# Layer 0's first head: four unread products in place of five, and its Toeplitz matrix loaded in two halves from two issuing engines

## The chip, the cores and the metric

The kernel runs on one core of a Trainium2 chip. The metric is the device time of one execution in microseconds (us); the time of a kernel is the median of its runs. "The profile" is one execution recorded by the hardware profiler: a page of sums, and a trace that can be asked for single instructions. Engines: PE is TensorE's matmul and PEld its weight load, DVE is VectorE, ACT is ScalarE, POOL is GpSimd, SP is SyncE. A "q" behind a name (SPq, ACTq) marks a DMA issue by that engine.

## The reference

An array x of 64 batches, 32 heads (positions) and 512 features goes through two layers, each a "conditioning" step and a feed-forward step that are added to x. The change touches only the conditioning step of layer 0, a long convolution along the 512 features with one kernel per head:

```python
def _get_kernel(log_dt, C, log_A_real, A_imag, length):
    Cc = C[..., 0] + 1j * C[..., 1]
    dt = jnp.exp(log_dt)
    A = -jnp.exp(log_A_real) + 1j * A_imag
    dtA = A * dt[:, None]
    P = dtA[:, :, None] * jnp.arange(length, dtype=jnp.float32)
    Cs = Cc * (jnp.exp(dtA) - 1.0) / A
    K = 2.0 * jnp.einsum('hn,hnl->hl', Cs, jnp.exp(P)).real
    return K
...
u_m = u * mask[:, None, :]
kernel = _get_kernel(log_dt, C, log_A_real, A_imag, Lq)
...
y = jnp.fft.irfft(u_f * k_f, n=n)[..., :Lq]
y = y + u_m * D[:, None]
return y * mask[:, None, :]
```

After it come a mixture of low-rank adapters beside a dense product (layer 0's feed-forward), a gated layer with adapters per batch (layer 1's conditioning) and a mixture of 16 experts with a shared one (layer 1's feed-forward).

## The kernel before, in words

All arithmetic is float32. x lies in SBUF transposed (`xall`, features on partitions), and layer 0 works on it in four blocks `tb` of eight heads each.

*The convolution kernels.* For each block of heads the 512 values of the kernel of each head are made from exponentials and sines (class `Kernels`: `decays`, `angles`, `weighed` on VectorE and ScalarE), then a small product per head on TensorE (`products`, L329). `to_memory` copies the result out of PSUM (L334), adds D to the first value (L336) and stores it in a DRAM tensor `kpad` with a DMA that ScalarE issues (L338). A row of `kpad` is 127 zeros and the 512 values. The first block is split: `early` makes heads 0 to 5, `second` heads 6 and 7.

*The unread products.* Between them stand five products of 128 x 512 (L400) whose result nobody reads; they are written into `ps_mm`, the PSUM pool that the convolutions use too. A float32 product of this kernel is recorded as two weight loads and two matmuls ("passes").

*The convolution.* `convolved(tb, hl, yT)` loads for two heads at a time the Toeplitz matrices `g` (L495): partition p of head h reads 512 values of `kpad` that begin at p. Heads 0 and 1 come as two loads of 256 KB, later pairs as one of 512 KB; the tile has three buffers. Then head h's product y is four matmuls, one for each block d of 128 columns of g (L511), and VectorE multiplies y with the length mask into `yT` (L518). Behind each head come two steps of the next block's kernels (the first is `decays`, L306 and L307). After eight heads `by_tokens` (L528) and the main products (L589) take yT.

*What sets the order.* Inside `tc.manual_schedule(engines=by_hand)` the instructions of PE, DVE and Activation keep the order in which they are written, DMA issues included. SP and POOL are put in order by the scheduler. The written order around the change is: `early.products()`, `early.to_memory()`, the angles of `second`, the unread products, `second.products()`, `second.to_memory()`, and then, in the loop over `tb`, `convolved(0, 0, yT)`.

Of the kernel before, what the change touches and what calls it, by code (L numbers as in the profile page):

```python
# [17 lines left out]
P = 128  # L18
B, H, L = 64, 32, 512
# [15 lines left out]
KW = 640  # L35
# [68 lines left out]
def kernel(ctx: ExitStack, tc: tile.TileContext, a: dict, out: bass.AP):  # L104
    nc = tc.nc
# [11 lines left out]
    def bank(pool, name):  # L117
        return pool.tile([P, TB], F32, tag="bank", name=name)
# [62 lines left out]
    kpad = dram.tile([H, KW], F32, name="kpad")  # L181
# [14 lines left out]
    def fetch(n):  # L196

        g, j = divmod(n, NF)
        blocks[n] = stream.tile([P, 7 * BW], F32, tag="w", name=f"w_{n}")
        if g == 0:  # L200
            nc.sync.dma_start(blocks[n][:, 0 : 4 * BW], a["cw"][j])
        else:
            nc.sync.dma_start(blocks[n][:, 0 : 3 * BW], a["cw"][j][:, 0 : 3 * BW])
            nc.sync.dma_start(blocks[n][:, 3 * BW :], sums_d[j])
# [191 lines left out]
        ts(mlen[:, j, :], intf[:, 0, :], col(C_L + j), None, ALU.is_gt)  # L396
    run(second.weighed())

    for _ in range(5):
        mm(bank(ps_mm, "unread"), ident, xT[0][:, 0, :], start=True, stop=True)  # L400
    second.products()
    second.to_memory()
# [70 lines left out]
    with tc.tile_pool(name="l0", bufs=1) as l0, tc.tile_pool(name="l0b", bufs=2) as l0b:  # L473
# [10 lines left out]
        def convolved(tb, hl, yT):  # L484

            h = tb * HB + hl
            if h % 2 == 0:
                g = l0b.tile([P, 2, L], F32, tag="g", name=f"g_{h}", bufs=3)  # L490

                for i, n in ((0, 1), (1, 1)) if h == 0 else ((0, 2),):
                    src = kpad.offset + (h + i) * KW
                    src = bass.AP(tensor=kpad.tensor, offset=src, ap=[[1, P], [KW, n], [1, L]])
                    load = nc.sync.dma_start(g[:, i : i + n, :], src)  # L495
                if hl == HB - 2 and tb > 0:
                    with tc.issue_after(load.ins):
                        for n in ((0, 1), (2, 3), ())[tb - 1]:
                            fetch(n)
                        for j in range((tb - 1) * 4, min(tb * 4, NF)):  # L500
                            nc.sync.dma_start(wn[:, j, :, TW : TW + L // 2], a["cn"][j])
                if h == HB - 2:
                    with tc.issue_after(load.ins):
                        for later in range(1, NTB):
                            nc.sync.dma_start(xT[later], a["xT"][later])
                toeplitz.append(g)
            g = toeplitz[-1]
            y = bank(ps_mm, f"y_{h}")
            cols = slice(hl * B, (hl + 1) * B)
            for d in range(NC):  # L510
                mm(  # L511
                    y[:, d * B : NC * B],
                    g[:, h % 2, d * P : (d + 1) * P],
                    xT[tb][:, 0 : NC - d, cols],
                    start=(d == 0),
                    stop=(d == NC - 1),
                )
            tt(yT[:, :, cols], y[:, 0 : NC * B].rearrange("p (c b) -> p c b", b=B), mlen, ALU.mult)  # L518
            if tb in (1, 2):
                coming[0].rows(1)  # L520
# [80 lines left out]
        for tb in range(NTB):  # L601
# [7 lines left out]
            for hl in range(HB):  # L609
                convolved(tb, hl, yT)  # L610
                next(steps, None)
                next(steps, None)
                if hl == 1 and tb > 0:
                    counted(tb - 1)
                if tb == NTB - 1:
                    for j in range(hl, NF, HB):
                        columns(0, j)
# [328 lines left out]
    for g in range(NG):  # L946
# [3 lines left out]
        for j in range(NF):  # L950
# [6 lines left out]
            if j % 4 == 0:  # L957
                lo = adapters[:, 0 : min(4, NF - j)]
# [592 lines left out]
```

## Time and profile before

| | |
|---|---|
| median of 3 runs | 1020.14 us (1019.03 to 1020.51) |
| the profiled execution | 1020.05 us |
| its span, first to last instruction | 1018.3 us |
| mean granted TensorE clock | 1.000 |
| busy: PE, DVE, ACT, POOL | 987.4, 648.3, 212.0, 170.1 us |
| bytes moved by DMA | 190.62 MB, mean 187 GB/s |

The profiled execution's time is 1.75 us longer than its span; that is what lies around the first and the last instruction. Times inside the trace are counted from the span's start. A line of the timeline gives start, length, engine, line of the code, operation, what is written and read, shapes, how often in a row, and in brackets how long the engine had been idle and what ended that. Matmuls are pipelined, so their lengths overlap; the distance between starts is the better measure of their pace. DMA lines give the size of one transfer and the median time from its issue to its landing.

### The profile page before, as it was taken

The page shows a single profiled execution, that of the slowest core. Times are in us where ns is not written, and L with a number is a line of the kernel's source. Part 1 is how long each engine was busy: PE and PEld are TensorE (multiplying, and loading weights), DVE is VectorE, ACT ScalarE, POOL GpSimd, SP SyncE. Part 2 cuts the span into 40 slices and gives each one's busy share as a digit, 9 for nine tenths or more (in the row PEclk, how much of TensorE's full clock was granted, in tenths as well). Part 3 has the DMA queues.
Part 4 walks back from the last instruction along what each step waited for, and adds up shares of the span by engine and source line. Part 5 has one row for each costly group of instructions (what it writes and reads, how often), then busy time and mean ns, then how long its engine had stood idle before and what let it go on. Part 6 is the DMA issues. An engine that isn't in the chain of part 4 may idle for free. (4 is left out here: it accounts for less than half of the span.)

```text
span 1018.3 us, 16926 instructions
## 1 busy us (share of the span) xinstructions
PE 987.4 (97%) x6256; PEld 792.2 (78%) x6256; DVE 648.3 (64%) x1974; ACT 212.0 (21%) x439; POOL 170.1 (17%) x189
## 2 busy tenths in 40 slices
PE   3999999999999999999999999999999999999998
PEld 1777656888988889988889888897767677776665
DVE  6656567887666776766676767765765353333775
ACT  2322111121221311213212122121201222221100
POOL 2131001210301202102012021000000333331730
PEclk9999999999999999999999999999999999999999
DMA  6566408685665646746567557540940455555652
GB/s 187 191 224 232 136 21 301 236 294 174 224 199 192 238 164 213 248 161 214 186 198 257 175 189 238 172 141 17 409 188 1 133 167 166 166 165 199 200 176 95
DMA packets 64210, 190.62 MB, mean 187 GB/s; under 512 B 8512, under 2 KB 11616, under 8 KB 63488
## 3 DMA queue, kind: packets, MB, share of 16 engines
q1 hardware_dynamic: 49360, 138.30, 39.2%
q0 software_dynamic: 14176, 51.16, 16.2%
q8 instruction: 52, 0.85, 0.3%
q14 instruction: 30, 0.25, 0.1%
q10 hardware_dynamic: 592, 0.07, 0.1%
HBM read 158.35 MB, written 31.15 MB: 186 GB/s over the span
## 5 line engine op out<-in xcount | busy, mean ns | idle before, releaser
L885 PE MATMUL zp<-wn,at 128*128 128x288 f32 x704 | 185.4, 406 | 0.4 <-DVE at L984 0.4
L819 PE MATMUL gu<-t,w 128*128 128x128 f32 x1056 | 150.1, 278 | 0.9 <-DVE gus L966 0.9
L885 PEld LDWEIGHTS zp<-wn,at 128*128 128x128 f32 x704 | 127.1, 190 | 28.6 <-DVE at L984 0.6
L819 PEld LDWEIGHTS gu<-t,w 128*128 128x128 f32 x1056 | 135.4, 192 | 14.8 <-DVE gus L966 6.4
L444 POOL DMA_INDIRECT wa<-in_la,row_a x64 | 61.2, 956 | 299.9 <-issue 183.4
L982 ACT ACTIVATE si<-gus 128x256 f32<-128x256 f32 x88 | 36.7, 417 | 350.5 <-DVE gus L980 350.5
L819 PE MATMUL gum<-xall,w 128*128 128x128 f32 x704 | 93.0, 275 | 0.0
L819 PEld LDWEIGHTS gum<-xall,w 128*128 128x128 f32 x704 | 85.7, 192 | 0.0
L1327 PE MATMUL egu<-wall,zx 128*128 x336 | 80.6, 383 | 0.4 <-issue 0.4
L966 DVE TENSOR_TENSOR gus<-gu,los 128x512 f32<-128x512 f32 x88 | 60.6, 688 | 28.7 <-PE gu L819 26.2
L960 DVE TENSOR_TENSOR los<-los 128x512 f32<-128x512 f32 (+1 forms) x72 | 46.6, 647 | 49.9 <-ACT los L839 48.3
L1327 PEld LDWEIGHTS egu<-wall,zx 128*128 128x128 f32 x336 | 60.5, 189 | 20.0 <-ACT zx L1318 13.0
L984 DVE TENSOR_TENSOR at<-si,gus 128x256 f32<-128x256 f32 x88 | 37.4, 425 | 48.2 <-ACT si L982 48.2
L1308 POOL DMA_INDIRECT zr<-zd,tok x42 | 39.7, 946 | 159.4 <-PE zrp L1316 86.3
L839 ACT COPY los<-lo 128x512 f32<-128x512 f32 (+1 forms) x96 | 46.6, 560 | 60.1 <-PE lo L836 60.1
L1099 PE MATMUL op<-sat,sw 128*128 128x512 f32 x128 | 58.0, 595 | 0.6 <-DVE sat L1124 0.3
L589 PE MATMUL main<-yT,w 128*128 128x512 f32 x128 | 58.4, 599 | 0.0
L836 PEld LDWEIGHTS lo<-rs,wb 64*128 64x128 f32 x704 | 42.6, 187 | 16.0 <-issue 10.6
L836 PE MATMUL lo<-rs,wb 64*128 64x128 f32 x704 | 48.0, 279 | 6.1 <-DVE gus L980 5.5
L819 PE MATMUL gum<-t,w 128*128 128x128 f32 x352 | 53.7, 275 | 0.0
L819 PE MATMUL gu<-xall,w 128*128 128x128 f32 x352 | 53.7, 275 | 0.0
L1347 DVE COPY eys<-ey 128x512 f32<-128x512 f32 x42 | 29.1, 692 | 29.7 <-PE ey L1345 29.7
(316 smaller groups left out, 1452.0 us busy)
## 6 DMA issues: line engine op xcount, KB each, us to landing
w<-sums_d SPq DMA_DIRECT2D x77, 512.0 KB, 4.8
w<-in_cw SPq DMA_DIRECT2D x77, 384.0 KB, 3.4
wall<-in_xw SPq DMA_DIRECT2D x16, 768.0 KB, 15.1
yd<-eys SPq DMA_DIRECT2D x42, 256.0 KB, 2.8
g<-kpad SPq DMA_DIRECT2D x15, 512.0 KB, 5.5
w<-in_cw SPq DMA_DIRECT2D x11, 512.0 KB, 4.7
sums_d<-w SPq DMA_DIRECT2D x9, 512.0 KB, 3.6
xall<-in_xT SPq DMA_DIRECT2D x4, 1024.0 KB, 8.6
```

The lines of the kernel that those rows point to most:

```text
L444: nc.gpsimd.indirect_dma_start(to, None, src, at)
L589: mm(ps, w0[:, c, o * P : (o + 1) * P], yT[:, c, :], start=(c == 0), stop=(c == NC - 1),)
L819: mm(to, block(n, i)[:, c * P : (c + 1) * P], x[:, c], start=(c == 0), stop=(c == 1))
L836: mm(banks[which][:, at : at + P], wb[mine, lo : lo + P], r[mine, half, :], start=True, stop=True)
L839: nc.scalar.copy(to[:, first - j : first - j + n, 2 * which : 2 * which + 2], src)
L885: mm(self.zp[half][s][:, 0 : DW - TW], at[:, 1 - half, :], wn[:, j, s, lo : lo + DW - TW], start=(j == 0), stop=(j == NF - 1),)
L960: tt(lo[:, :, i], lo[:, :, i], lo[:, :, less], ALU.subtract)
L966: tt(flat, ps, adapters[:, j % 4].rearrange("p k t -> p (k t)"), ALU.add)
L984: tt(at, si, flat[:, TG:], ALU.mult)
L1099: mm(op[o], sw[j][:, i : i + P], at, start=(j == 0), stop=(j == NS1 - 1))
L1308: nc.gpsimd.indirect_dma_start(zr, None, zd[:, :], bass.IndirectOffsetOnAxis(ap=tok[:, t : t + 1], axis=0))
L1327: mm(ps[:, 0:256], x[:, c, :], wflat()[:, bass.ds(start + c * 256, 256)], start=(c == 0), stop=(c == NC - 1))
```

## The change

One unread product fewer; and head 0's matrix, one load of 256 KB by SP before, becomes two loads of 128 KB: columns 0 to 255 issued by SP, columns 256 to 511 issued by ScalarE. Head 1's load and all later ones stay as they are.

```diff
-    for _ in range(5):
+    for _ in range(4):
         mm(bank(ps_mm, "unread"), ident, xT[0][:, 0, :], start=True, stop=True)
     second.products()
     second.to_memory()
...
                 for i, n in ((0, 1), (1, 1)) if h == 0 else ((0, 2),):
                     src = kpad.offset + (h + i) * KW
                     src = bass.AP(tensor=kpad.tensor, offset=src, ap=[[1, P], [KW, n], [1, L]])
+                    if h == 0 and i == 0:
+
+                        half = L // 2
+                        for queue, lo in ((nc.sync, 0), (nc.scalar, half)):
+                            src = bass.AP(tensor=kpad.tensor, offset=kpad.offset + lo, ap=[[1, P], [KW, 1], [1, half]])
+                            queue.dma_start(g[:, 0:1, lo : lo + half], src)
+                        continue
                     load = nc.sync.dma_start(g[:, i : i + n, :], src)
```

## The prediction

> **What bounds the kernel now.** I read the page first, then the timeline of 15 to 50 us by engine, the waits, and the DMA issues with their landings. The page:
>
> ```profile
> span 1018.3 us, 16926 instructions
> ...
> PE 987.4 (97%) x6256; PEld 792.2 (78%) x6256; DVE 648.3 (64%) x1974; ACT 212.0 (21%) x439; POOL 170.1 (17%) x189
> ```
>
> TensorE (PE) is busy in 987.4 of 1018.3 us, and 16.0 of the idle 30.9 us lie before its first matmul. So a microsecond won or lost on PE early in layer 0 should reach the end. The change lies in PE's first 10 us. Timeline, PE (start, length, what):
>
> ```profile
> 16.01 0.80 PE L329 MATMUL kp<-kgen 128*16 128x32 f32 x12 [16.01 <-DVE intf L392]
> 16.74 7.00 PE L400 MATMUL unread<-xall,cst 128*128 128x512 f32 x10
> 23.66 0.29 PE L329 MATMUL kp<-kgen 128*16 128x32 f32 x4
> 23.89 9.84 PE L511 MATMUL y<-xall,g 128*128 128x256 f32 x64
> ```
>
> Five products are ten passes (two each). Then come the four small products of heads 6 and 7 (`second`), then head 0's convolution (y), without a gap. The weight loads on PE show how fast the passes ran:
>
> ```profile
> 21.17 0.33 PEld L400 LDWEIGHTS unread<-xall,cst 128*128 128x128 f32 x1 [0.52 <-issue]
> 21.86 0.19 PEld L400 LDWEIGHTS unread<-xall,cst 128*128 128x128 f32 x1 [0.36 <-issue]
> 22.29 0.19 PEld L400 LDWEIGHTS unread<-xall,cst 128*128 128x128 f32 x1 [0.24 <-PE unread L400]
> 22.71 0.19 PEld L400 LDWEIGHTS unread<-xall,cst 128*128 128x128 f32 x1 [0.24 <-issue]
> 23.66 0.17 PEld L329 LDWEIGHTS kp<-kgen 128*16 128x16 f32 x4 [0.76 <-issue]
> ```
>
> Up to about 21.7 us passes start 0.855 us apart (18.60, 19.46 in the timeline), from there 0.43 apart (22.28, 22.71): the last four run twice as fast as the first, though the granted clock stands at 1.00 in every window.
>
> ScalarE (ACT) is in hand-written order, and this view decides:
>
> ```profile
> 17.41 0.34 ACTq L338 DMA_DIRECT2D kpad<-kgen  x1
> 19.07 0.61 ACT L273 ACTIVATE kgen<-kgen,cst 128x32 f32<-128x32 f32 x2 [6.17 <-DVE kgen L272]
> 24.42 0.31 ACTq L338 DMA_DIRECT2D kpad<-kgen  x1
> 24.76 1.28 ACT L307 ACT_TABLE_LOAD   x1 [5.08 <-DVE kgen L336]
> ```
>
> The second L338 is `second.to_memory()`'s store. It waits for VectorE (L334, L336), which waits for the products at 23.66, and whatever follows in ACT's order waits behind it: the table load of L307 idles 5.08 us for L336.
>
> The Toeplitz load itself: SyncE's (SP's) first issue, and how long loads take from issue to landing (last column):
>
> ```profile
> 18.98 0.33 SPq L495 DMA_DIRECT2D g<-kpad  x1
> ```
>
> ```profile
> g<-kpad SPq DMA_DIRECT2D x1, 256.0 KB, 3.4
> ```
>
> ```profile
> g<-kpad SPq DMA_DIRECT2D x2, 256.0 KB, 3.6
> ...
> cst<-in_cst SPq DMA_DIRECT2D x1, 177.5 KB, 2.5
> s<-in_s SPq DMA_DIRECT2D x1, 80.0 KB, 1.9
> ```
>
> Head 0's matrix lands at 18.98 + 3.4 = 22.4 us; y starts at 23.89, so it waits for nothing.
>
> **Fewer products.** Two passes go. The first eight are as before, so 2 x 0.43 = 0.86 us leave PE's queue. Products of `second` start at 23.66 - 0.86 = 22.80, y at 23.88 - 0.86 = 23.02. The whole matrix landed at 22.4, so this edit alone would be worth the full -0.86 us, with no wait in its place.
>
> **First half on SP.** One issue replaces one, so SP's other loads keep their places. Half the bytes land at 22.4 or before, and y starts at 23.02: worth nothing. Its cover is 0.6 us.
>
> **Second half on ACT.** `convolved(0, 0)` is traced behind `second.to_memory()` and before the decays of L307, and ACT keeps the written order. So this DMA leaves not at 18.98 but right behind the store. With the 0.86 us taken off: L334 at 23.99 becomes 23.13, L336 23.38, the store 23.56; the next instruction on ACT came 0.34 us later (24.76 - 24.42), hence issue at 23.90. Behind it on ACT is the table load of L307, which becomes 0.86 - 0.34 = 0.5 us earlier than before all the same: nothing.
>
> The trace has no such load. From below: 80 KB on an idle queue, 1.9 us. From above: the 256 KB loads of the same memory, 3.6. By bytes between the 80 and 177.5 KB rows, 128 KB take 1.9 + 0.6 x 48/97.5 = 2.2; but this load has 128 rows read from the same few KB as head 0's (3.4), and from 22 to 25 us SP's loads fill the engines (DMA share 0.97 to 1.07 in the windows). I take the middle of 2.2 and 3.4, 2.8: landing at 26.70, between 25.80 and 27.50. A gain is excluded: even 1.9 is too late.
>
> Head 0's y runs over four column blocks d. Blocks 0 and 1 need the first half: weight loads from 23.88, block 2's at 24.75, hence 0.87 us. After the change PE is through with them at 23.02 + 0.87 = 23.89 and stands until 26.70, some 2.8 us. Block 2 then starts 26.70 - 24.75 = 1.95 us later than before (1.05 to 2.75). Everything on PE is behind it: y of heads 1 to 7, the token products, the main products; VectorE's L518 waits for y in turn.
>
> **What is late next.** Heads 6 and 7's load waits for the buffer of heads 0 and 1 (issue 26.54, behind y of head 1), and lands 3.9 us later, at 30.4; their y starts near 31.3. Both ends move with head 1, so the 0.9 us between them stays. VectorE is idle 0.2 to 0.3 us ahead of each of the last L518, waiting for y, so it moves along too. Later loads are started by buffers that PE frees. I see nothing tied to absolute time that would swallow the delay, and count it whole.
>
> [...] The rows: SP alone moved 375 GB/s at full DMA share by 23 us, but 152 GB/s at a share of 0.75 between 20 and 21. [...]
>
> The second: passes ran at half speed until 21.7 us, after 5.7 us of work, and the longest later stop by the waits of PE is this one (total, times, longest us), with no weight load of the big products above 0.192 us afterwards:
>
> ```profile
> PE lo L836 <- DVE gus L980: 5.5, 5, 1.3
> ```
>
> [...] I take no fall, and keep it as a case.
>
> **Sum.** -0.86 + (0.86 + 1.95) = +1.95 us on block 2 and all behind it. The profiled execution took 1020.05 (span 1018.3 and 1.75 around it), the median of the runs is 1020.14: 1022.0 and 1022.1. I predict 1022.1. A measurement of this kernel tells about 0.2%, 2.04 us, from no change; the forecast lies just inside.
>
> **Rivals.**
> 1. *The half isn't held* (not slower): ACT's DMA is put ahead of the store, or lands early enough. It decides if the half lands by 23.89 for the full gain, by 24.75 to break even, that is with an issue by about 22. ACT stands idle from 19.7, which speaks for it; the 5.08 us that L307 stood behind the store speaks against. Then -0.86: 1019.3. Chance 0.09.
> 2. *The clock falls back* during the stop: +1.95 + 1.7 to 3.4, 1023.8 to 1025.5. For it: the stop is twice the longest in the trace. Chance 0.20.
> 3. *Head 0 waits for both halves before block 0*, if the wait is kept by the whole tile: blocks 0 and 1 run behind the landing too, +0.87: 1022.9. Against: head 0's load at 18.98 did not wait for the store of other rows of kpad, so parts are told apart. Chance 0.07.
> 4. *The delay is swallowed* by a later wait: 1020.1. Against: PE's 97%. Chance 0.04.
>
> **How the numbers follow.** The likeliest, 0.60: 1021.2 to 1022.9; 2.04 us lies near its middle, so 0.28 of it is slower and 0.32 the same. Slower: 0.28 + 0.20 + 0.07 = 0.55. The same: 0.32 + 0.09 + 0.04, less 0.02 for a gain of rival 1 that measures larger: 0.43. Faster 0.02. The range 1020.3 to 1025.2 leaves out rivals 1 and 4 and the top of rival 2, 0.18 together.
>
> **What would show it.** Right: eight unread passes, y's first weight load near 23.0, then PE idle over 2 us within head 0 for the DMA g<-kpad, an ACT-queue load of 128 KB issued near 23.9 behind L338. The landing column gives the disputed 2.8. Weight loads of 0.33 us behind the stop would show rival 2; y's first load near 26.7, rival 3. An ACT issue before 22 us would make the prediction wrong, as would y without a gap; a gap in head 0 with the later stages at their old times would mean rival 4.

## The result, and the profile after

The changed kernel is slower: 1024.36 us (median of 7 runs, 1023.89 to 1025.98) against 1019.41 us (median of 7 runs of the kernel before), which is 4.95 us more, a ratio of 1.0043 with a 95% interval of 1.0032 to 1.0055. Its profiled execution took 1024.06 us, 4.01 more than the one of before. From the page after:

```profile
span 1022.3 us, 16926 instructions
...
PE 988.2 (97%) x6254; PEld 792.9 (78%) x6254; DVE 648.3 (63%) x1974; ACT 212.1 (21%) x439; POOL 169.3 (17%) x189
```

PE's work grew by less than a microsecond; its span grew by four. The same first microseconds of PE's timeline (start, length, what):

```profile
16.73 5.26 PE L400 MATMUL unread<-xall,cst 128*128 128x512 f32 x8
21.93 0.29 PE L329 MATMUL kp<-kgen 128*16 128x32 f32 x4
22.34 0.99 PE L518 MATMUL y<-xall,g 128*128 128x256 f32 x4
26.24 10.75 PE L518 MATMUL y<-xall,g 128*128 128x128 f32 x60 [2.91 <-DMA g<-kpad]
```

PE did four passes of head 0 (blocks 0 and 1), stood 2.91 us for the second half of the matrix, and then did the other 60 passes of the eight heads. ACT's timeline says why the half came late:

```profile
22.68 0.31 ACTq L338 DMA_DIRECT2D kpad<-kgen  x1
23.09 0.38 ACTq L500 DMA_DIRECT2D g<-kpad  x1
23.50 1.28 ACT L307 ACT_TABLE_LOAD   x1 [3.82 <-DVE kgen L336]
```

It was issued at 23.09, right behind the store of heads 6 and 7, 4.1 us after SP issued the first half at 19.01. The DMA issues (how many, size of each, us to landing):

```profile
g<-kpad SPq DMA_DIRECT2D x1, 128.0 KB, 3.2
g<-kpad ACTq DMA_DIRECT2D x1, 128.0 KB, 3.1
kpad<-kgen ACTq DMA_DIRECT2D x1, 4.0 KB, 3.3
```

And the stretches of one microsecond, whose granted clock stands behind the comma that follows the first number:

```profile
26.00:27.00 1.00, 0.76 (x5) 0.76 (x6) 0.03 (x1) 0.00 (x0) 0.00 (x0) 0.87 0.00 0
27.00:28.00 1.00, 1.00 (x3) 0.82 (x3) 1.00 (x3) 0.11 (x1) 0.00 (x0) 0.50 0.00 0
...
30.00:31.00 1.00, 1.00 (x8) 0.96 (x7) 0.43 (x2) 0.00 (x0) 0.00 (x0) 0.92 0.57 127
```

Each row gives the stretch, its length, the busy time of PE, PEld, DVE, ACT and POOL, then the clock, the DMA share and GB/s: 0.87, 0.50 and 0.92. In finer stretches the clock falls to half at 26.76 us, half a microsecond after PE went on, and comes back at 30.17. It was not this execution alone: the mean granted clock was 0.998 in six of the seven runs and 0.996 in one, and 3.41 us at half speed in a span of 1022 make 0.998.

So the first stage, from PE's first product to the first token product, took 20.83 us (16.00 to 36.83), not 17.55 (16.01 to 33.56). Block 2 of head 0 began at 26.24, not 24.75: 1.49 us. From there to the first token product it took 10.59 us, not 8.81: 1.78 us, nearly all of it the half clock (3.41 us at half speed lose 1.7). These two are 3.27 of the 4.01 us. The other 0.7 came in far behind, 0.3 us in the adapter stage and 0.4 in the expert stage; what they are, no run here settled.

### The profile page after: what moved, and what is told of

The parts are those of the page before. It is cut to its first block, busy times and chain, and to the rows that moved or that the text cites. A ratio compares the mean times of both kernels' runs of the same rounds, so it can differ in the third digit from the quotient of the medians.

```text
span 1022.3 us, 16926 instructions
## 1 busy us (share of the span) xinstructions
PE 988.2 (97%) x6254; PEld 792.9 (78%) x6254; DVE 648.3 (63%) x1974; ACT 212.1 (21%) x439; POOL 169.3 (17%) x189
```

## The experiments

They ran on chips where the kernel before takes 1032 to 1033 us and single runs spread over 10 us. In their traces the clock also falls to half for one or more stretches of 3.41 us further on in the kernel (with halves by SP the mean granted clock is 0.99 in each of 300 to 500, 500 to 700 and 700 to 1000 us, and one fall is at 627.04), each worth up to 1.7 us (half of 3.41, an estimate), and not the same ones in every trace (with one filler 0.99 in the last of these alone). Whole times settle little there, so the first stage, from PE's first product to the first token product, is read from each trace, and the ratio to the kernel before (95% interval) stands beside it.

"Whole" is one load of head 0's matrix by SP, "halves" are two, and a filler is an unread product written behind the store of heads 6 and 7. A stop "ahead of it" lies before head 0, not inside it.

| kernel | stop in head 0, us | half clock, us | first stage, us | ratio |
|---|---|---|---|---|
| before | none | none | 17.55 | 1 |
| changed | 2.91 | 26.76 to 30.17 | 20.83 | 1.0043 (1.0032, 1.0055) |
| changed again | 3.05 | 28.82 to 32.23 | 21.85 | 1.0035 (1.0014, 1.0057) |
| four whole | none | none | 16.77 | 1.0003 (0.9989, 1.0017) |
| five, halves | 2.92 | 28.56 to 31.97 | 22.45 | 1.0048 (1.0029, 1.0068) |
| store by POOL | 0.26 | none | 18.25 | 1.0003 (0.9989, 1.0018) |
| store behind head 0 | 0.44 | none | 18.10 | 1.0025 (1.0011, 1.0039) |
| halves by SP | 0.39 | none | 17.48 | 1.0002 (0.9984, 1.0020) |
| one filler | 2.88 | 26.26 to 33.09 | 22.46 | 1.0052 (1.0036, 1.0069) |
| two fillers | 1.98 | none | 19.49 | 1.0039 (1.0015, 1.0062) |
| three fillers | 0.44 | none | 19.32 | 1.0035 (1.0020, 1.0050) |
| three whole | 1.26 ahead of it | none | 16.41, then 16.93 | 1.0007 (0.9993, 1.0021), 0.9998 (0.9974, 1.0021) |
| none whole | 1.22 ahead of it | begins at half | 17.83 | 0.9997 (0.9978, 1.0016) |

The stage holds one thing that no edit set: the moment at which the clock first comes up (read from the weight loads of L400). In the kernel before that was 5.7 us behind PE's first product, and within about 0.5 us of this in "changed again", "four whole", "five, halves", both rows with the store moved and the second "three whole". In "changed", "halves by SP", the three rows with fillers and the first "three whole" it was 1.5 to 2.6 us earlier, which can shorten a stage by half as much (an estimate from passes 0.855 us apart before that moment and 0.43 behind it).

**Each part alone.** Four products, one load:

```diff
-    for _ in range(5):
+    for _ in range(4):
         mm(bank(ps_mm, "unread"), ident, xT[0][:, 0, :], start=True, stop=True)
```

> Four unread products, head 0's matrix in one load by SP as before: one part of the change alone. Theory (the half on ACT is held behind the store of heads 6 and 7, PE stops 2.9 us inside head 0, and that stop lets the array's clock fall to half for one window of some 3.2 us): without the half on ACT there is no stop and no half clock; y starts 0.86 us earlier than with five products if the clock comes up at the same moment, so the time is 0.9 us below the kernel before, about 1019.2 where that takes 1020.1. Rival (four products are too few to hold the clock, whatever the load does): half clock for some 3 us behind 23 us here too, 1 to 2.5 us above the kernel before.

The first stage took 16.77 us, 0.78 less, without a stop or half clock, as the theory said. The whole time doesn't resolve 0.8 us (interval -0.11% to +0.17%). PE's timeline has no gap:

```profile
23.09 0.29 PE L329 MATMUL kp<-kgen 128*16 128x32 f32 x4
23.31 9.84 PE L511 MATMUL y<-xall,g 128*128 128x256 f32 x64
```

Five products, with the halves (the changed kernel with `range(5)`):

> Five unread products, head 0's matrix in halves by SP and ACT: the other part alone. Theory: the store on ACT waits for the products behind the fifth unread one, so all of it moves 0.86 us later than in the changed kernel: half issued 0.78 us behind the end of second's products, landing 3.15 us later, a stop of about 2.9 us in head 0, half clock for one window; 0.9 us above the changed kernel when the clock comes up at the same moment, about 1025. Rival (the fall of the clock comes from having only four products): the stop stays, the clock does not fall, some 1.7 us less, 1023.2 to 1023.5.

The stop was 2.92 us, the half clock lasted 3.41 us, and the first stage came out 4.9 us above the kernel before. The rival falls: the number of products does not make the clock fall, the stop does.

**The place on ACT.** The store of heads 6 and 7 is given to POOL:

```diff
-            nc.scalar.dma_start(to, ksb[:NA])
+            (nc.gpsimd if hs.start == HB - 2 else nc.scalar).dma_start(to, ksb[:NA])
```

> The changed kernel with the store of heads 6 and 7 issued by POOL, not by ACT, so that nothing on ACT stands ahead of the half but two sines that end at 19.7 us. Theory: ACT issues the half at about 19.7 to 20, it lands by about 23.2, y waits at most a few tenths of a us, no half clock; 0.5 to 0.9 us below the kernel before. Rival (a load on ACT's queue is late by itself, from the queue or from short rows beside SP's loads, not from what it is held behind): the half still lands behind 25 us, the stop stays at 2 us or more, the time within 1 us of the changed kernel.

Neither expectation came true as a whole. ACT issued the half at 19.52, and the stop shrank to 0.26 us, so the store had held it. But the half landed only near 24.3, 4.7 us after its issue, and the first stage took 0.70 us more than before. 0.62 us of that stood ahead of head 6, whose load waited for the store, now POOL's. To take that mix apart, `second.to_memory()` was left on ACT and written behind head 0's convolution:

```diff
     second.products()
-    second.to_memory()
...
                 convolved(tb, hl, yT)
+                if tb == 0 and hl == 0:
+                    second.to_memory()
```

> The changed kernel with second.to_memory() written behind head 0's convolution, so that on ACT the half stands ahead of the store. Theory: ACT issues the half at 19.5 us; it shares the engines with SP's loads and lands near 24.3, as it did with the store on POOL; a stop of 0.3 us in head 0, none in front of head 6, no half clock; first stage 17.0 to 17.2 us, time 0.4 to 0.5 below the kernel before. Rival (it is ACT's queue that makes the half late): landing behind 25.5 us wherever it stands, first stage above 18.5.

The landing is as expected, the stage is not: 18.10 us, 0.55 above the kernel before, and the time is 0.25% above it. ACT's issue, and PE's weight loads of blocks 2 and 3:

```profile
19.32 0.37 ACTq L499 DMA_DIRECT2D g<-kpad  x1
```

```profile
24.12 0.52 PEld L517 LDWEIGHTS y<-xall,g 128*128 128x128 f32 x4 [0.44 <-DMA g<-kpad]
```

The 128 KB issued by ACT at 19.32 landed near 24.1, 4.8 us later; in the kernel before all 256 KB issued by SP at 18.98 were there at 22.4. Beside SP's queue of 1.4 MB the second queue made its half later, not earlier. The next stop, 0.43 us, was ahead of head 6. SP's waits (total, times, longest us) show that head 6's load stood for the store:

```profile
SPq L501 <- DMA kpad<-kgen: 3.4, 1, 3.4
```

This edit had made that store later (issued at 25.57, the load at 27.60; 24.42 and 26.54 in the kernel before). So these 0.43 us may belong to the experiment and not to the split, and so may the 0.62 us with the store on POOL. Without them the two stages would be 17.67 and 17.63 us (estimates from these numbers), still 0.1 above the kernel before: with the hold gone, the split takes back at least what the fifth product gives, and wins nothing. The rest of the 0.25% in the whole time stays open.

Both halves by SP (`((nc.sync, 0), (nc.sync, half))`):

> The changed kernel with both halves issued by SP, one behind the other. Read on the first stage, from the first product on PE to the first token product (gt), which is 17.55 us in the kernel before and 20.83 in the changed one. Theory (only the half's place on ACT costs): no stop in head 0, no half clock, first stage 16.7 to 16.9, time 0.8 us below the kernel before. Rival (halves are slow by themselves, with 128 short rows each, or the extra issue makes SP's other loads late): a stop of 0.3 us or more in head 0 or in front of head 1.

The rival's mark, 0.3 us, was passed: 0.39 us for the second half, 0.16 ahead of head 1, 0.74 ahead of head 6. Here the clock came up some 2 us earlier than in the kernel before, so y began at 22.07, ahead of its loads; the stage is as long as before. What stood ahead of head 6 is shown by SP's waits:

```profile
SPq L502 <- DMA kpad<-kgen: 3.6, 1, 3.6
```

The load of heads 6 and 7 went out at 26.79, when the 4 KB store had landed (1.6 us after its issue in the kernel before, with SP's loads nearly done, 3.3 in the changed kernel). With the 3.9 us of before it lands at 30.7, and head 6 began at 31.07; the trace names VectorE for that last wait, so this step is argued from the times, not shown. A front that gets faster meets this load next.

**The stop and the clock.** Three unread products behind the store fill the stop:

```diff
     second.products()
     second.to_memory()
+    for _ in range(3):
+        mm(bank(ps_mm, "unread"), ident, xT[0][:, 0, :], start=True, stop=True)
```

> The changed kernel with three more unread products behind second's store, ahead of head 0's convolution: the half lands as late as in the changed kernel, but PE works for 2.6 of the 2.9 us. Theory: the load's lateness alone stays, 1.5 us against the kernel before, and the clock does not fall; 2.5 us below the changed kernel in spite of the added work, about 1021.5 to 1021.9. Rival (the clock falls whether PE stands or not, or the time is lost elsewhere): the time stays at the changed kernel's 1024.

```profile
22.58 2.84 PE L404 MATMUL unread<-xall,cst 128*128 128x512 f32 x6
25.25 0.92 PE L520 MATMUL y<-xall,g 128*128 128x256 f32 x4
26.62 9.18 PE L520 MATMUL y<-xall,g 128*128 128x128 f32 x60 [0.44 <-DMA g<-kpad]
```

The half came as late (26.6), PE worked instead of standing, the clock held, and the 60 passes took 9.18 us, not 10.75. The first stage is 1.77 us above the kernel before: the lateness, without the half clock. More work made a shorter stage than in the changed kernel. In whole times its interval overlaps those of the kernels with half clock, so this is shown for the stage alone.

How long a stop is too long? One filler and two fillers:

> The changed kernel with one more unread product behind second's store, so that PE stops for about 2.1 us and not 2.9. Theory A (the clock falls when PE has stood for the better part of a window of about 3.4 us, and 2.1 is short of that): no half clock, first stage about 19.2 us, 1.6 above the kernel before. Theory B (a window in which PE works less than about half is enough): half clock behind the stop for one window, first stage 20.5 to 21.0 as in the changed kernel.

> The changed kernel with two unread products behind second's store: a stop between the 2.9 us of no filler and the 0.4 of three, some 1.3 to 2 us by where the half lands. Theory (the clock is set at the end of fixed windows of 3.41 us by how much PE worked in the window; 0.32 of a window was too little, and three fillers were enough): with over half of each window worked, no fall; first stage 19.2 to 20.0 us. Rival (any stop of over 1.3 us lets the clock fall): half clock for one or two windows, first stage 20.8 or more.

With one, the stop did not shrink (2.88 us): the clock had come up early, at 19.4, so the half was asked for at 23.00, while SP's loads were still running, and landed 3.8 us later. The clock was at half for 6.83 us (26.26 to 33.09). With two, the stop was 1.98 us and the clock held. And the changed kernel once more:

> The changed kernel once more, beside the others on one chip, to see whether the clock falls at another place of its windows: theory (a stop of 2.9 us leaves so little of one window that it falls wherever the windows lie), half clock for 3.41 or 6.83 us, the fall a whole number of 3.41 us behind the moment at which the clock came up, first stage 20.5 to 22.5 us. Rival (it fell only for the windows of the one execution): no half clock, first stage about 19.1 us.

It fell again, for 3.41 us, and the stage was 4.3 us above the kernel before: 2.5 for block 2's later start and 1.8 behind it. What the falls have in common shows when the time is cut where the clock changed. The rows below are stretches of 3.41 us, one fence for each kernel, columns as above. Changed kernel, changed again and one filler: the clock fell at the end of the first row of each; in one filler's second row it was at half and stayed there.

```profile
23.35:26.76 3.41, 0.52 (x5) 0.52 (x5) 0.00 (x0) 1.28 (x1) 0.00 (x0) 1.00 0.62 232
```

```profile
25.41:28.82 3.41, 1.53 (x11) 1.48 (x12) 0.84 (x3) 0.44 (x1) 0.00 (x0) 1.00 0.13 40
```

```profile
22.85:26.26 3.41, 1.09 (x5) 0.57 (x3) 0.00 (x0) 1.28 (x1) 0.00 (x0) 1.00 0.87 316
26.26:29.67 3.41, 2.84 (x10) 2.67 (x11) 1.36 (x3) 0.52 (x1) 0.00 (x0) 0.50 0.00 1
```

And two fillers, where it held:

```profile
22.76:26.17 3.41, 1.86 (x7) 0.95 (x5) 0.00 (x0) 1.28 (x1) 0.00 (x0) 1.00 0.82 302
```

Half clock lasted 3.41 us three times and 6.83 once, and each fall lies 6.83 us, two such stretches, behind the moment at which the clock had come up, as closely as the weight loads of L400 tell it (where they go from 0.34 to 0.19 us). PE had worked 15%, 45% and 32% of the stretch before a fall, and 20% with five products and halves; with 54% it held. With one filler, half clock went on behind a stretch that PE had worked to 83%, and ended behind a full one. The falls did not lie at one place: 26.26, 26.76, 28.56 and 28.82 us.

Does PE's share alone tell a fall? Two stretches further on, with the row behind each: halves by SP, where the clock fell after 57%, and one filler, where it held after 49%.

```profile
623.63:627.04 3.41, 1.93 (x24) 1.71 (x24) 2.66 (x13) 1.26 (x5) 0.33 (x1) 1.00 0.82 336
627.04:630.45 3.41, 3.41 (x17) 3.36 (x16) 2.30 (x8) 1.05 (x2) 0.61 (x1) 0.50 0.55 192
```

```profile
964.93:968.34 3.41, 1.67 (x8) 0.98 (x6) 0.00 (x0) 0.00 (x0) 2.69 (x3) 1.00 0.73 211
968.34:971.75 3.41, 0.00 (x0) 0.00 (x0) 0.76 (x2) 0.00 (x0) 0.15 (x1) 1.00 0.47 143
```

It does not: a stretch with more work was followed by half clock, and one with less was not. So that the clock held in two fillers, with 54%, is not assured for another execution, and what share brings it back was not shown either: the 83% and the full stretch are two rows of one trace. How a stop lies in the stretches counts too. Cut in the middle, one of 2.9 us would leave 57% of work in each of two (an estimate from these numbers), which need not be a fall: with 54% it held in two fillers, with 57% it fell in halves by SP.

**What the unread products are for.** Three of them, one load, twice:

> Three unread products and head 0's matrix in one load by SP. Theory (the products fill the time until the matrix lands, 3.4 us behind its issue at 19.0): y comes up at 22.1 to 22.4, the matrix lands at 22.4 to 22.6, a stop of at most 0.4 us, no half clock; first stage 16.0 to 16.4 us, time 1.2 to 1.5 below the kernel before. Rival (fewer than four products bring the clock up late or let it fall): weight loads of 0.33 us within y, first stage 17 us or more.

> Three unread products and one load by SP, once more, for the time of the whole kernel, which the first run left open: first stage 16.3 to 16.6 us, and with it 1.1 us or 0.1% below the kernel before. Rival (the gain is given back behind the first stage): ratio 1.000 or above with the first stage as short.

The first time the clock came up early and PE stood 1.26 us for the matrix; the second time it came up late, and 0.71 us were lost ahead of head 6, whose load went out at 26.18. The stage is 0.6 to 1.1 us shorter than in the kernel before; the whole time is not shown to be faster. And none at all:

> No unread product, head 0's matrix in one load by SP: what the products are there for. Theory (they keep the array's clock up until the matrix lands): PE stands from 16.8 to 20.8 us for second's factors, does four small products, stands again until 22.4 for the matrix and begins the convolution at half clock, for one to two windows of 3.4 us; y begins 1.5 us earlier than in the kernel before and loses 1.7 to 3.4 us, first stage 17.8 to 19.5 us against 17.55. Rival (they are only in the way): no half speed after 26 us, first stage 16.1 us.

```profile
20.88 0.37 PE L329 MATMUL kp<-kgen 128*16 128x32 f32 x4 [4.05 <-DVE kgen L324]
22.47 11.55 PE L509 MATMUL y<-xall,g 128*128 128x256 f32 x64 [1.22 <-DMA g<-kpad]
```

y began at 22.47, for the matrix, and its 64 passes took 11.55 us against 9.84: 1.7 us lost to the half clock (PE ran 4 to 6 passes of y a microsecond from 23 to 26 us and 9 from there), 1.4 won at the start, a stage 0.28 us longer. So in these single traces five products are worth 0.3 us against none, and less than nothing against three.

## Why the prediction was right or wrong

- *Direction and range*: slower was forecast as likeliest (0.55), and the range held the time. The likeliest case, 2.0 us more with no fall of the clock, did not come; the second rival did, given 0.20, with 1023.8 to 1025.5. No run of the kernel before shows the 1.7 to 3.4 us in that sum; in their place the runs of the change showed half clock for 3.41 us, worth 1.78 us in the profiled execution, and once, with one filler, for 6.83 us. That the rival's lower sum comes so near is in part luck: in the profiled execution an early rise of the clock made block 2's delay 0.46 us smaller than forecast, and 0.7 us of unknown cause made up for it.
- *Fewer products, -0.86 us*: right. With four products alone the stage was 0.78 us shorter. In the profiled execution of the changed kernel y began 1.5 us earlier, since the clock also came up earlier (19.9, not 21.7); in the changed kernel's second trace it came up at 22.0.
- *The half is held behind the store on ACT*: right. Issue 0.41 us behind the store's, where 0.34 was taken.
- *First half on SP, cover 0.6 us*: no stop, but hardly any cover. With the early clock the half landed at 22.2 (19.01 + 3.2) and its first weight load came at 22.31.
- *Landing 2.8 us after issue (1.9 to 3.6)*: 3.1, within the bounds. The stop of 2.8 us was 2.91.
- *Block 2 1.95 us later*: 1.49 in the profiled execution, 2.53 in the second trace (27.28), where the clock came up at about the moment it did in the kernel before. Right in kind, 0.6 us too small there, half of it the landing.
- *"I take no fall"*: this is the step that failed. It was a choice of mine; no trace I had showed what follows a stop of 2.8 us. In the first stages the clock fell after stretches of 3.41 us in which PE still worked 15% to 45%, and, further on in halves by SP, after one of 57%. A stop of 2.9 us left 45% or less in all four traces that had it. The fall cost 1.78 us in the profiled execution. That no weight load after the stop of 1.3 us takes more than 0.192 us holds but for one (L785, 0.241 us, where half speed shows as 0.33), and it only said that stops of up to 1.3 us did no harm here.
- *The whole delay reaches the end*: right, and 0.7 us more, unexplained.
- *A second issuing engine, no term in the sum*: right for the changed kernel, where the store held the half. But where ACT issued the half unheld, it came 1.7 us later (24.1) than the whole matrix had by SP (22.4).
- *Rivals 1, 3 and 4*: none came. Blocks 0 and 1 ran ahead of the stop, so the wait is kept by parts of the tile.

## What to carry to other kernels

Before a DMA is moved to a second engine, look what stands ahead of it in that engine's order and when that is done: here a 4 KB store, waiting for PE itself, held half of a matrix by 4 us. Price a stop of PE twice: its length, and the stretch at half clock that may follow; here a stop of 2.9 us, most of a stretch of 3.41, was followed by it four times of four and cost 1.7 us or more on top. And when a front gets faster, ask which load, timed by something else, it meets next.

## What the runs showed that I had not expected

- In four first stages the clock fell 6.83 us behind the moment at which it had come up, and stayed at half for 3.41 us or, once, 6.83. In the 3.41 us ahead of the fall PE had worked 15%, 20%, 32% and 45%; with 54% it held, and further on it fell after 57% and held after 49%.
- The granted clock reads 1.00 from the start, although passes ran 0.855 us apart, at half speed, until it came up: only falls after that are in the rows. Until then the spacing of the passes is the clock.
- A 4 KB store took 1.6 us to land with SP's loads nearly done and 3.3 with SP's loads running and the half behind it; a 128 KB load beside them took 4.8.
